# One product 128 rows deep in place of two passes 64 rows deep, in a graph kernel's walk over edge buckets

## The chip, the cores and the metric

The kernel runs on one core of a Trainium2 chip. The metric is the device time of one execution in microseconds (us); of several executions the median is given.

## What is computed

A small graph network over 3125 nodes with 256 features and 53125 directed edges: a message-passing layer, a mixture of expert layers, two averaging graph convolutions, and a last feed-forward layer on selected tokens. Only the first layer matters here:

```python
node_i = node_features[i_idx]
node_j = node_features[j_idx]
msg_input = jnp.concatenate([node_i, node_j, edge_features], axis=-1)
h = jax.nn.relu(msg_input @ mW1 + mb1)
messages = h @ mW2 + mb2
aggregated = jax.ops.segment_sum(messages, i_idx, num_segments=node_features.shape[0])
...
u = jax.nn.relu(update_input @ uW1 + ub1)
updated = u @ uW2 + ub2
return node_features + updated
```

For each edge the hidden vector of 512 elements is a sum of three parts: what the source node gives, what the destination node gives, and what the edge's 16 attributes give.

## The kernel before

A first stage (up to 645 us) sorts the edges into buckets by source node. A bucket is 32 nodes (`BN`), there are 98 buckets (`NBK`), and four buckets make a group. `rows` holds a group's edges, five rounds of 128 edges for each of the four buckets. An edge's row has 68 elements: 32 that mark its source node within the bucket (one of them is 1), 32 for its attributes (16 rounded ones and 16 remainders), and four with indices.

The first stage also makes tables. `tab_b` holds what each node gives as a destination. `tab_h` holds what it gives as a source, split in two halves, `[node, 2, 512]`: a part rounded to the TensorE format float32r, and the remainder. `w_h` holds the attributes' weights, split in the same way. The kernel adds the products with both halves.

The second stage, `edges_by_bucket` (665 to 1860 us), walks 25 groups of five rounds: 125 steps. A step treats four buckets, 128 edges of each:

- `fetch` (L713, GpSimd, called POOL in the profile) gathers each edge's row of `tab_b` into `cb`, one indirect DMA per bucket. It is issued three steps ahead.
- `turned` (L735) turns the first 64 elements of each edge's row on TensorE, so that they lie along the partitions: product with an identity matrix into the PSUM tile `pt`. ScalarE then copies them into `oT` in SBUF (the helper `copy`, L107). It is issued one step ahead of `spread`.
- `spread` (L752) multiplies `oT` with `gives`, a tile that holds the source parts of the bucket's 32 nodes and the 32 rows of attribute weights. The result goes into two PSUM tiles `pa`, two buckets in each. This is where the two passes are: `c` runs over the two halves of the table.
- `hidden_units` (L758, VectorE) adds `pa` to `cb`; `relu` (L763, ScalarE) follows.
- `by_source` (L769) sums the hidden vectors by source node into the PSUM tile `ph`.

Buckets with an even number lie on partitions 0 to 63 of `gives` and `oT`, those with an odd number on partitions 64 to 127. `begin` loads `gives` for the next group, once in five steps, from the SyncE queue; there are two such tiles. The weights' rows of both are loaded once, ahead of the loop (L842).

Between these parts the loop takes one piece at a time of two other jobs: `counts` (one-hot tiles on VectorE at L791 and L795, products at L810, tiles `cn` stored to `adj_h`), and `finish_nodes`, the rest of the layer and the experts for two finished groups of nodes. The latter spans ten steps, so the pattern of the stage repeats every ten. The order on TensorE, VectorE, ScalarE and SyncE is the order written in the program (`manual_schedule`). The PSUM tiles of `turned`, `counts` and `finish_nodes` come in turn from one ring of three banks (`bank`). L506, L521, L524, L531, L546, L556, L619, L635, L639 and L649 are products of `finish_nodes`; L133 is a transpose of it, L777 closes a group.

The remaining stages (from 1860 us) are the two convolutions, with products at L1277, and the last layer.

Of the kernel before, what the change touches and what calls it, by code (L numbers as in the profile page):

```python
# [8 lines left out]
F32 = mybir.dt.float32  # L9
F16 = mybir.dt.float16  # L10
F32R = mybir.dt.float32r
# [5 lines left out]
P = 128  # L17
N, E, D, HID = 3125, 53125, 256, 512
# [5 lines left out]
GB = 4  # L24
# [10 lines left out]
BN, NBK = 32, -(-N // 32)  # L35
# [7 lines left out]
RW = AT_DST + 1  # L43
# [7 lines left out]
def gnn_ffn_kernel(ctx: ExitStack, tc: tile.TileContext, a: dict, out: bass.AP):  # L51
    nc = tc.nc
# [12 lines left out]
    def bank(name):  # L65
        return rings[-1].tile([P, 512], F32, tag="bank", name=name)
# [7 lines left out]
    ident_r = const.tile([P, P], F32R, name="ident_r")  # L74
# [31 lines left out]
    def copy(dst, src):  # L106
        nc.scalar.activation(dst, src, AF.Copy)  # L107
# [40 lines left out]
    tab_h = dram.tile([NP, 2, HID], F32, name="tab_h")  # L148
    w_h = dram.tile([32, 2, HID], F32, name="w_h")
# [311 lines left out]
    def rest_of(fast):  # L461
# [211 lines left out]
        def edges_by_bucket():  # L673
            with tc.tile_pool(name="bk", bufs=2) as bp, tc.tile_pool(name="upd", bufs=2) as up, \
# [5 lines left out]
                for hf, w in ((half0, W0), (half1, W1)):  # L680
                    left = NP - NBK * BN
                    flat = hf[NBK * BN:, :].rearrange("s (h l) -> (s h) l", l=w)
# [4 lines left out]

                gives = [bp.tile([P, 2, 2, HID], F32R, name=f"gives{i}", bufs=1) for i in range(2)]  # L690

                def begin(g):
                    nb = min(4, NBK - 4 * g)
                    ag = gives[g % 2]
                    for i in range(2):
                        src = bass.AP(tensor=tab_h.tensor, offset=tab_h.offset + (g * P + i * BN) * 2 * HID,
                                      ap=[[2 * HID, BN], [4 * BN * HID, nb // 2], [1, 2 * HID]])
                        nc.sync.dma_start(ag[2 * BN * i:2 * BN * i + BN, :nb // 2].bitcast(F32).rearrange("p i c h -> p i (c h)"), src)
                    rows = bp.tile([P, PER, RW], F32R, name="rows", bufs=3)
                    nc.sync.dma_start(rows.bitcast(F32).rearrange("p r w -> p (r w)"),  # L700
                                      cbuf[g * P * PER:(g + 1) * P * PER, :].rearrange("(p r) w -> p (r w)", p=P))
                    return dict(g=g, nb=nb, m=nb * BN, ag=ag, rows=rows, oa={}, ob={})
# [24 lines left out]
                def turned(u, r):  # L727

                    pt = bank("pt")
                    pairs = u["nb"] // 2  # L730
                    flat = u["rows"].rearrange("p r w -> p (r w)")
                    for j in range(u["nb"]):

                        at = (GB * r + j) * RW - j % 2 * 2 * BN
                        nc.tensor.matmul(pt[:, j * P:(j + 1) * P], lhsT=flat[:, at:at + P], rhs=ident_r, start=True, stop=True)  # L735
                    oT = bp.tile([P, 2, P], F32R, name="oT", bufs=2)
                    got = pt.rearrange("p (i k e) -> p i k e", i=2, k=2)
                    for k in range(2):
                        rows = slice(k * 2 * BN, (k + 1) * 2 * BN)
                        copy(oT[rows, :pairs], got[rows, :pairs, k])  # L740
                    return oT

                def spread(u, oT):

                    got = []
                    for j in range(0, u["nb"], 2):
                        pa = pA.tile([P, 2, HID], F32, name="pa")
                        got.append(pa)
                    for c in range(2):
                        for j in range(u["nb"]):  # L750
                            at = slice(j % 2 * 2 * BN, (j % 2 + 1) * 2 * BN)
                            nc.tensor.matmul(got[j // 2][:, j % 2, :], lhsT=oT[at, j // 2, :], rhs=u["ag"][at, j // 2, c, :],  # L752
                                             start=c == 0, stop=c == 1)
                    return got

                def hidden_units(u, cb, pas):
# [72 lines left out]
                def step(i):  # L829
                    g, r = steps[i]  # L830
                    return units[g], r

                def ahead_of(i):
                    if i < len(steps):
                        g, r = steps[i]
                        cbs[i] = fetch(units[g], r)

                units[0] = begin(0)
                for t in gives:
                    for at in (BN, 3 * BN):  # L840
                        for i in range(2):
                            nc.sync.dma_start(t[at:at + 32, i].bitcast(F32), w_h[:])  # L842

# [2 lines left out]
                for i in range(3):  # L848
                    ahead_of(i)
                hs = hidden_units(units[0], cbs[0], spread(units[0], turned(*step(0))))  # L850
                relu(hs, 0), relu(hs, 1)
                leaving(units[0])
                oT = turned(*step(1))
                for i, (g, r) in enumerate(steps):
                    u, more = units[g], i + 1 < len(steps)
                    coming = []
                    if more:
                        v = step(i + 1)
                        coming = hidden_units(v[0], cbs[i + 1], spread(v[0], oT))
# [7 lines left out]
                    if i + 2 < len(steps):  # L867
                        oT = turned(*step(i + 2))
                    take(tally)
                    relu(coming, 1)  # L870
                    if r == 0 and g + 1 < NB:
                        units[g + 1] = begin(g + 1)
# [170 lines left out]
        if fast:  # L1043
            edges_by_bucket()
        else:
            with ExitStack() as es:
                ring(es)
                with tc.tile_pool(name="keys", bufs=1) as kp:
                    edges_by_scatter(kp)
                st["up"] = es.enter_context(tc.tile_pool(name="upd", bufs=2))  # L1050
                for k0, nb in PAIRS:
                    got = []
                    for k in range(k0, k0 + nb):
                        hs = st["up"].tile([P, HW], F32, name="h0")
                        nc.sync.dma_start(hs, hsum[k * P:(k + 1) * P, :])
                        got.append(hs)
                    for _ in finish_nodes((k0, nb), got):
                        pass
            rings.pop()
# [231 lines left out]
        with tc.tile_pool(name="ffn", bufs=2) as fp, tc.tile_pool(name="rank", bufs=1) as rp:  # L1291
            wrow = rp.tile([P, NP], F32, name="wrow")
            for k0, nb in GROUPS:
                pt = bank("ptw")
# [5 lines left out]
            for k in range(NB):  # L1300
                w = wcol[:, k:k + 1]
# [13 lines left out]
            for k0, nb in GROUPS:  # L1315
# [5 lines left out]
                for i in range(nb):  # L1321
                    k = k0 + i
                    py = bank("py")
                    for m in range(8):
                        nc.tensor.matmul(py[:, :D], lhsT=gT[:, m, i * P:(i + 1) * P], rhs=fw2[:, m, :],  # L1325
                                         start=m == 0, stop=m == 7)
# [4 lines left out]
                    rows = min(P, N - k * P)  # L1331
# [50 lines left out]
```

## Time and profile before

| | |
|---|---|
| Time, median of 3 runs | 2401.82 us (2400.23 to 2407.05) |
| Profiled execution: its own time | 2503.9 us |
| Profiled execution: span | 2501.8 us |
| Mean granted TensorE clock over the span | 0.832 |
| PE busy | 1836.7 us (73%) |
| VectorE (DVE) busy | 1549.4 us (62%) |
| GpSimd (POOL) busy | 987.6 us (39%) |
| ScalarE (ACT) busy | 876.3 us (35%) |
| L752, PE | 980 products, busy 188.7 us |
| L735, PE | 490 products |
| L107 oT, ACT | 250 copies, busy 93.1 us, mean 373 ns |

In the profile PE is TensorE, and PEld its loading of the stationary operand. A row reads: source line, engine, operation, tile written and tiles read, shapes, count; then busy time and the mean time of one instruction, from its start to its end. Products overlap in the array, so the busy time of a group divided by its count can be well below the mean of one. In a timeline the first number is the start of a group in us from the start of the span, and the second is the time that it covers. In a list of waits the numbers are the total in us, how many there were, and the longest.

### The profile page before, as it was taken

The numbers are of one execution on the slowest core, as the hardware profiler recorded it, in microseconds if no ns is written. First come the engines' busy times: TensorE is split into PE (matmuls) and PEld (weight loads), VectorE is DVE, ScalarE is ACT, GpSimd is POOL, SyncE is SP. The second block draws the span as 40 slices with busy tenths as digits, with TensorE's granted clock in tenths as the row PEclk, the third lists the DMA queues.
The fourth block names the chain that finished last, engine by engine and source line by source line (L and its number), as shares of the span: only waits on it lengthen the run. The fifth ranks groups of instructions, "written<-read, shape, count | busy, mean of one in ns | idle before, by whom it ended". The sixth has DMA issues, their size and how long they took to land. (4 is left out here: it accounts for less than half of the span.)

```text
span 2501.8 us, 26233 instructions
## 1 busy us (share of the span) xinstructions
PE 1836.7 (73%) x7873; PEld 1091.7 (44%) x7873; DVE 1549.4 (62%) x4427; ACT 876.3 (35%) x1553; POOL 987.6 (39%) x1032
## 2 busy tenths in 40 slices
PE   3455551111078898898898998898885999999689
PEld 1222220000034454455454454454454777886356
DVE  7687775555255665665665665665644676667931
ACT  1211110000045555555555555554433333343111
POOL 4566666766545444445444444444300000110000
PEclk9687775555568889889889899899897999999889
DMA  8233330000666556555555555555304444650000
GB/s 265 96 129 124 119 118 25 25 24 26 167 201 196 146 159 173 161 162 178 157 158 165 150 178 165 149 172 169 114 26 125 120 129 119 169 145 1 0 34 19
DMA packets 231403, 309.98 MB, mean 124 GB/s; under 512 B 34392, under 2 KB 165315, under 8 KB 230884
## 3 DMA queue, kind: packets, MB, share of 16 engines
q1 hardware_dynamic: 167296, 153.00, 20.8%
q0 software_dynamic: 52512, 142.96, 19.6%
q10 hardware_dynamic: 11444, 12.27, 1.6%
q8 instruction: 64, 1.05, 0.2%
q14 instruction: 87, 0.71, 0.1%
HBM read 226.44 MB, written 81.69 MB: 123 GB/s over the span
## 5 line engine op out<-in xcount | busy, mean ns | idle before, releaser
L713 POOL DMA_INDIRECT cb<-tab_b,goes_to x490 | 477.4, 974 | 617.8 <-issue 275.1
L394 POOL DMA_INDIRECT cbuf<-rt,to x416 | 416.3, 1001 | 233.3 <-issue 197.1
L758 DVE TENSOR_TENSOR cb<-pa,cb 128x1024 f32<-128x1024 f32 x245 | 288.7, 1218 | 263.2 <-PE pa L752 190.1
L1277 PE MATMUL padj<-z,slab 128*128 128x512 f32 x1250 | 321.4, 410 | 16.0 <-DVE z L1186 16.0
L763 ACT ACTIVATE cb<-cb 128x1024 f32<-128x1024 f32 x245 | 257.6, 1051 | 94.7 <-DVE cb L758 72.9
L1277 PEld LDWEIGHTS padj<-z,slab 128*128 128x128 f32 x1250 | 233.2, 192 | 75.4 <-issue 24.1
L752 PE MATMUL pa<-gives,oT 64*128 64x512 f32 x980 | 188.7, 506 | 36.1 <-ACT oT L107 34.3
L133 PE MATMUL pt<-ident,xn 128*128 128x128 f32 x200 | 49.5, 339 | 218.8 <-DVE xn L122 130.3
L363 PE MATMUL pk<-oh,later 128*128 128x392 f16 x104 | 47.2, 454 | 190.3 <-DVE oh L340 95.0
L810 PE MATMUL pn<-ob,oa 128*128 128x448 f16 (+1 forms) x692 | 165.6, 363 | 20.6 <-ACT cn L107 7.5
L125 POOL TENSOR_TENSOR x<-x,xn 128x256 f32<-128x256 f32 x25 | 24.4, 978 | 352.7 <-DVE xn L122 352.7
L795 DVE TENSOR_SCALAR ob<-ids,rows 128x448 f16<-128x448 f16 (+1 forms) x490 | 163.3, 333 | 0.0
L791 DVE TENSOR_SCALAR oa<-ids,rows 128x128 f16<-128x128 f16 x692 | 163.0, 262 | 0.0
L752 PEld LDWEIGHTS pa<-gives,oT 64*128 64x128 f32 x980 | 105.8, 231 | 101.2 <-ACT oT L107 43.8
L769 PE MATMUL ph<-cb,rows 128*32 128x512 f32 x980 | 144.8, 645 | 0.0
L107 ACT ACTIVATE oT<-pt 64x256 fp32r<-64x256 f32 (+1 forms) x250 | 93.1, 373 | 134.9 <-DMA cb<-tab_b,goes_to 72.2
L107 ACT ACTIVATE cn<-pn 128x352 f16<-128x352 f32 x196 | 98.3, 502 | 118.0 <-PE pn L810 91.0
L313 PE MATMUL pp<-mw,xTa 128*128 128x512 f32 x200 | 133.1, 826 | 0.2 <-issue 0.2
L133 PEld LDWEIGHTS pt<-ident,xn 128*128 128x128 f32 x200 | 24.8, 160 | 243.1 <-DVE xn L122 129.5
L107 ACT ACTIVATE rt<-row 128x144 f32<-128x144 f32 x104 | 32.8, 319 | 258.7 <-DMA cbuf<-rt,to 208.1
L506 PE MATMUL pd<-xT,fw 128*128 128x512 f32 (+1 forms) x224 | 91.8, 566 | 35.4 <-DVE y L1328 35.4
L735 PEld LDWEIGHTS pt<-ident_r,rows 128*128 128x128 f32 x490 | 67.1, 198 | 110.4 <-issue 69.4
(221 smaller groups left out, 3137.4 us busy)
## 6 DMA issues: line engine op xcount, KB each, us to landing
two<-adj_h SPq DMA_DIRECT2D x24, 1600.0 KB
rows<-cbuf SPq DMA_DIRECT2D x25, 680.0 KB
gives<-tab_h SPq DMA_DIRECT2D x48, 256.0 KB
adj_h<-cn SPq DMA_DIRECT2D x98, 112.0 KB
adj_h<-cn SPq DMA_DIRECT2D x98, 88.0 KB
cb<-tab_b,goes_to POOLq DMA_INDIRECT x490
cbuf<-rt,to POOLq DMA_INDIRECT x416
cbuf<-empty ACTq DMA_DIRECT2D x4, 1632.0 KB
```

The source lines that it names most:

```text
L107: nc.scalar.activation(dst, src, AF.Copy)
L313: nc.tensor.matmul(pp, lhsT=xT[:, c, :], rhs=mw1[:, 2 * h + c, :], start=c == 0, stop=c == 1)
L394: one_of = nc.gpsimd.indirect_dma_start(out=cbuf[:], out_offset=bass.IndirectOffsetOnAxis(ap=to[:n, i:i + 1], axis=0), in_=rt[:n, i, :], i ...
L713: nc.gpsimd.indirect_dma_start(out=cb[:, j, :], out_offset=None, in_=tab_b[:], in_offset=bass.IndirectOffsetOnAxis(ap=u["to"][:, i:i + 1], ...
L752: nc.tensor.matmul(got[j // 2][:, j % 2, :], lhsT=oT[at, j // 2, :], rhs=u["ag"][at, j // 2, c, :], start=c == 0, stop=c == 1)
L758: nc.vector.tensor_tensor(cb[:, j:j + 2], pa, cb[:, j:j + 2], op=OP.add)
L763: nc.scalar.activation(h, h, AF.Relu)
L769: nc.tensor.matmul(u["ph"][j * BN:(j + 1) * BN, :], lhsT=u["rows"][:, GB * r + j, :BN].bitcast(F32), rhs=hs[j // 2][:, j % 2, :], start=r ...
L791: nc.vector.tensor_scalar(oa, ids[:, 1 + i * P:1 + (i + 1) * P], field[:, 0:1], None, op0=OP.is_equal)
L795: nc.vector.tensor_scalar(ob[:, :w], ids[:, 1:w + 1], field[:, 1:2], None, op0=OP.is_equal)
L810: nc.tensor.matmul(pn[:, :w], lhsT=u["oa"].pop((j, r, i)), rhs=u["ob"][j, r][:, :w], start=r == rs[0], stop=r == rs[-1])
L1277: nc.tensor.matmul(pa, lhsT=slab[:, c, :], rhs=(z2 if second else z1)[:, c, :], start=c == 0, stop=c == NB - 1)
```

## The change

The two halves of the source part now lie below each other: the rounded half with its attribute weights on partitions 0 to 63, the remainder half with its own on partitions 64 to 127, for each of the four buckets. `oT` holds a bucket's 64 turned elements twice, once in each half of the partitions. One product 128 rows deep then adds both halves.

```diff
-gives = [bp.tile([P, 2, 2, HID], F32R, name=f"gives{i}", bufs=1) for i in range(2)]
+gives = [bp.tile([P, GB, HID], F32R, name=f"gives{i}", bufs=1) for i in range(2)]
 def begin(g):
     nb = min(4, NBK - 4 * g)
     ag = gives[g % 2]
-    for i in range(2):
-        src = bass.AP(tensor=tab_h.tensor, offset=tab_h.offset + (g * P + i * BN) * 2 * HID,
-                      ap=[[2 * HID, BN], [4 * BN * HID, nb // 2], [1, 2 * HID]])
-        nc.sync.dma_start(ag[2 * BN * i:2 * BN * i + BN, :nb // 2].bitcast(F32).rearrange("p i c h -> p i (c h)"), src)
+    for c in range(2):
+        src = bass.AP(tensor=tab_h.tensor, offset=tab_h.offset + (g * P * 2 + c) * HID,
+                      ap=[[2 * HID, BN], [2 * BN * HID, nb], [1, HID]])
+        nc.sync.dma_start(ag[2 * BN * c:2 * BN * c + BN, :nb].bitcast(F32), src)
...
 def turned(u, r):
     pt = bank("pt")
-    pairs = u["nb"] // 2
-    flat = u["rows"].rearrange("p r w -> p (r w)")
-    for j in range(u["nb"]):
-        at = (GB * r + j) * RW - j % 2 * 2 * BN
-        nc.tensor.matmul(pt[:, j * P:(j + 1) * P], lhsT=flat[:, at:at + P], rhs=ident_r, start=True, stop=True)
-    oT = bp.tile([P, 2, P], F32R, name="oT", bufs=2)
-    got = pt.rearrange("p (i k e) -> p i k e", i=2, k=2)
-    for k in range(2):
-        rows = slice(k * 2 * BN, (k + 1) * 2 * BN)
-        copy(oT[rows, :pairs], got[rows, :pairs, k])
+    nb = u["nb"]
+    for j in range(nb):
+        nc.tensor.matmul(pt[:2 * BN, j * P:(j + 1) * P], lhsT=u["rows"][:, GB * r + j, :2 * BN], rhs=ident_r,
+                         start=True, stop=True)
+    oT = bp.tile([P, GB, P], F32R, name="oT", bufs=2)
+    for c in range(2):
+        copy(oT[2 * BN * c:2 * BN * (c + 1), :nb], pt[:2 * BN, :nb * P].rearrange("p (j e) -> p j e", e=P))
     return oT
 def spread(u, oT):
...
-    for c in range(2):
-        for j in range(u["nb"]):
-            at = slice(j % 2 * 2 * BN, (j % 2 + 1) * 2 * BN)
-            nc.tensor.matmul(got[j // 2][:, j % 2, :], lhsT=oT[at, j // 2, :], rhs=u["ag"][at, j // 2, c, :],
-                             start=c == 0, stop=c == 1)
+    for j in range(u["nb"]):
+        nc.tensor.matmul(got[j // 2][:, j % 2, :], lhsT=oT[:, j, :], rhs=u["ag"][:, j, :], start=True, stop=True)
...
 for t in gives:
-    for at in (BN, 3 * BN):
-        for i in range(2):
-            nc.sync.dma_start(t[at:at + 32, i].bitcast(F32), w_h[:])
+    for c, at in enumerate((BN, 3 * BN)):
+        nc.sync.dma_start(t[at:at + 32].bitcast(F32), w_h[:, c, :].unsqueeze(1).to_broadcast([32, GB, HID]))
```

## The prediction

> **What bounds the kernel now.** The change touches only the stage that walks the buckets of edges, so I looked there first. The windows view, cut at every tenth step of that stage, shows busy time by engine (the next numbers are granted TensorE clock, DMA share and GB/s):
>
> ```profile
> 692.00:757.00 65.00, 48.94 (x222) 23.93 (x222) 36.65 (x73) 31.88 (x50) 31.89 (x34) 0.68 0.65 194
> ...
> 1134.00:1228.00 94.00, 83.83 (x422) 47.45 (x420) 59.19 (x169) 49.20 (x89) 44.33 (x47) 0.90 0.55 167
> ```
>
> Ten steps take 94 us. PE is busy for 83.8 of them, DVE for 59.2, ACT for 49.2, POOL for 44.3. There are eleven such periods from 757 to 1795 us. Then the waits over these periods:
>
> ```profile
> POOL cb L713 <- ACT cb L763: 136.3, 30, 7.3
> DVE cb L758 <- PE pa L752: 136.9, 51, 5.9
> ...
> ACT cn L107 <- PE pn L810: 78.7, 11, 7.7
> ```
>
> DVE and ACT mostly wait for PE, and L752, the changed product, releases the longest of these waits. Only the first ten steps (692 to 757 us) are slack on PE. The chain that ended last is no help: its long pieces start at 1840 us, after this stage.
>
> The timeline of PE is the view that prices the change (start, busy us, then the group):
>
> ```profile
> 1289.54 0.61 PE L810 MATMUL pn<-ob,oa 128*128 128x352 f16 x3
> 1290.08 1.20 PE L752 MATMUL pa<-gives,oT 64*128 64x512 f32 x8
> 1291.21 1.13 PE L506 MATMUL pd<-sh,sw 128*128 128x256 f32 x4
> 1292.18 1.03 PE L506 MATMUL pd<-xT,ew 128*128 128x256 f32 x4
> ...
> 1294.13 0.67 PE L735 MATMUL pt<-ident_r,rows 128*128 128x128 f32 x4
> 1294.64 0.93 PE L810 MATMUL pn<-ob,oa 128*128 128x448 f16 x4
> 1295.50 0.65 PE L619 MATMUL pd<-e,ew 128*64 128x256 f32 x4
> ...
> 1301.85 0.94 PE L810 MATMUL pn<-ob,oa 128*128 128x448 f16 x4
> 1302.62 0.59 PE L635 MATMUL psh<-sw,sh 128*128 128x256 f32 x2
> ```
>
> Eight products of L752 hold PE for 1.13 us (1290.08 to 1291.21), 0.14 us each. The same width at full depth costs more: in the chain view L1277 runs like this,
>
> ```profile
> 2136.80 5.72 PE padj L1277 x25
> ```
>
> 0.229 us each. So the 64-deep products already run two at a time, in the upper and lower half of the array, and **the count of matmuls is not what is saved**. What is saved is the rest of the block.
>
> **What the Trainium skill says.** "TensorEngine Tiling (Array Packing)", Tiling Modes, Key Properties: tiles work in parallel, and changing the tiling mode drains TensorE. The trace agrees with both: the pairs above, and L810 x4 holding PE 0.77 us ahead of the full-width L635 but 0.86 us ahead of the 64-column L619. The page gives no price; 0.09 us is the trace's. "TensorE: Matmul & The Clock Gate", Part 2, step 1: weights load while the running product streams, and their loading depends on the column count, not on depth. The trace agrees: the first L506 group after L752 takes 1.13 us, the next, with its weights loaded ahead, 1.03. The same page, Part 1: idle time halves the TensorE clock. PEclk is 0.88 in most periods, and a block of L752 takes 2.01 us from start to start elsewhere (1339.43 to 1341.44).
>
> **The change part by part**, for one period of ten steps.
>
> 1. L752, 8 products 64 deep become 4 that are 128 deep. Before: 0.09 to 0.10 entry drain, 1.13 for the block and its exit drain, 0.10 for weights that the next group could not load ahead; 1.33 us. After: 4 x 0.229 = 0.92 with neighbours of the same shape. Saving 0.41 us. Where the next group is narrow itself (L769 or L619: three of ten steps) that exit stays, and 0.21 us is saved. Four of ten blocks run at half clock; doubling the clocked parts gives an estimated 0.6 and 0.3 us there. Over one period: three at 0.41, one at 0.37 (behind it come the short L521), two at 0.21, three at 0.6, one at 0.3 = **4.1 us**. Bounds: 2.5 us, if loads are not pulled ahead, to 5.
>
> 2. Order. Now pa of the first two buckets is complete after 6 of 8 products (three pair slots), then after 2 of 4. DVE's L758 starts 0.23 us (0.43 at half clock) earlier, beside the drain saved. This helps the steps where DVE leads; I count it only against item 4.
>
> 3. L735 turns 64 columns instead of 128. Four now take 0.51 us (1294.13 to 1294.64), 0.11 each, as long as a 128-column weight load. The LDWEIGHTS of L619, 64 columns, lasts 134 ns against 192 ns (median, by line), so about 0.055 us apiece, 0.22 for four, is the least. But 64 columns are another mode: PE enters one here already (from L769's 32 columns), but must leave it again: 0.09 plus weights exposed, about 0.08 (0.05 for 64 columns on entry). After L777, one step in five, the entry is new too. Net -0.45 us per period. Bounds: -1.0 (no drain), +1.5 (no shorter products, every drain paid).
>
> 4. oT: two ACT copies of 64x256 become two of 64x512. The price before and the nearest row:
>
> ```profile
> 1337.30 0.78 ACT L107 ACTIVATE oT<-pt 64x256 fp32r<-64x256 f32 x2 [1.46 <-PE pt L521]
> 1338.10 1.06 ACT L763 ACTIVATE cb<-cb 128x1024 f32<-128x1024 f32 x1
> 1339.18 0.60 ACT L107 ACTIVATE hT<-pt 128x512 f32<-128x512 f32 x1
> ```
>
> 0.78 becomes 1.2 us: +0.42 per step, 4.2 us of ACT per period, 49 to 53 us of 94. Mostly it lies beside PE's work: oT is wanted a step later. It shows where PE waits for ACT's queue. The PSUM ring has three banks, so the third group after L735 needs pt's bank back; L524 starts at 1338.13, just as oT ends. Such places per period: L524, L639, L133 after the norm, and L556 after xT (L556 waits 1.7 us). At two of them (L133, L556) the chain runs back through L758 to L752 and item 2 pays. I charge the two others, 0.8, and 0.2 for slack elsewhere in the ring: **+1.0 us**. Bounds: 0.4 to 2.5. Behind the longer copies queue the second relu (L763), cn and xT; L769, POOL's fetch into cb and L810 wait for these, and the relu has most of a step to spare.
>
> 5. SP: gives still comes by two DMAs per group of the same bytes, in pieces of 2 KB instead of 4. They are issued five steps (45 us) ahead; SP's issue took 0.38 us in the median and may double, with nothing but rows and adj_h behind it. Before the loop eight issues of w_h become four. They span 658 to 677 us, but the first oT comes at 691.7, when ACT has issued its last weights. Cost nothing, on that cover; were it gone, 2 us once, either way.
>
> 6. The same store for gives, 2 KB more per partition for oT: no time. The first ten steps go round a loop of L758, relu, oT and L752, 5.9 us a turn: -0.7 at L752 (half clock, first pa early) against +0.4 for oT, about -0.3 each, **-3 us** (0 to -6). The last five steps: -1.
>
> Sum: 11 x (-4.1 - 0.45 + 1.0) = -39; with -3 and -1, **-43 us**. The profiled execution took 2503.9 us (span 2501.8), 102 above the median of 2401.8. No view says where; the granted clock and the order of this stage would have to differ for its share to matter, so I carry the difference over unchanged: 2401.8 - 43 = 2359 us.
>
> **The rivals.**
>
> A. Half the products, half the time: L752 is busy 188.7 us, so -94, to 2308 us. For it: the group's size. Against it: 0.14 us apiece shows that the halves overlap. Chance 0.04.
>
> B. Given back to ACT's queue and the narrow L735. At the upper bounds of items 3 and 4, with 1 at its middle, a period changes by -4.1 + 1.5 + 2.5 = -0.1 us, and the time is 2397 to 2403. For it: three banks only, and ACT's copies run back to back in some steps (oT, cn, relu, cn, xT from 1318 to 1322). Against it: ACT is half idle. Chance 0.10.
>
> C, slower: **the clock**. Less work on PE with the same stalls means longer pauses beside the work, and PE's clock halves after pauses. In the first ten steps, with PE busy 75% by this view, the granted clock is 0.68; in the steady periods, at 89%, it is 0.90. PE's 84 us per period at 0.88 become 84 x 0.88/k. The gain of 3.55 us is gone at k = 0.844; at 0.80 a period costs 8.4 - 3.5 = +4.9 us, and the kernel some 50 more: 2450 us. Against it: what goes is mostly drain, time in which the array did nothing, and no stall is added beyond 0.42 us. Chance 0.11.
>
> **How the numbers follow.** The forecast (2359 us) has a chance of 0.75. Its own range: all of items 1 and 3 at their best, little given back: 11 x -5.0 - 6 = -61, 2341 us; items 3 and 4 near their worst together with 1: about -9, 2393 us. Taking in part of A and B, 2336 to 2396 leaves out some 2 in 10. About 0.3% (7 us) is what a measurement of this kernel can tell from no change: faster 0.79, all of the forecast and A; same 0.09, most of B; slower 0.12, C and the rest.
>
> **What would show it.** Right: L752 x490 with about 0.23 us from start to start, a period of some 90.5 us, L735 with 64 columns at some 0.06 us spacing, oT at 590 to 600 ns, PEclk at 0.87 or higher. Wrong: periods that stay at 94 us with PE waiting for oT at L506, L531 or L810 (B); PEclk under 0.845 in these windows (C); L752 spaced 0.33 us, its weights not loaded ahead.

## The result, and the profile after

| | before | after |
|---|---|---|
| Median of 4 runs each | 2404.14 us (2400.23 to 2407.05) | 2373.35 us (2370.18 to 2379.82) |
| Ratio | | 0.9876, 95% interval 0.9847 to 0.9905 |
| Profiled execution: its own time, span | 2406.98 us, 2404.8 us | 2376.09 us, 2374.0 us |
| Mean granted TensorE clock | 0.843 | 0.856 |

The change made the kernel 30.8 us faster by the medians; 43 were forecast. The profile of before in this table is a second one, taken later (`e0_before_again`): the first, with its span of 2501.8 us, comes from an execution that is no partner for this profile of after, as shown below. After's lines are numbered anew: `turned` is at L732, `spread` at L746, VectorE's add at L751, the relu at L756, `by_source` at L762, `counts` at L803.

The windows view of the kernel after gives the first ten steps and the eleven periods of ten steps together (length; busy time by engine; then granted clock, DMA share and GB/s):

```profile
638.30:691.30 53.00, 38.82 (x183) 17.14 (x183) 36.83 (x73) 34.34 (x48) 31.61 (x34) 0.78 0.78 244
691.30:1671.30 980.00, 845.84 (x4173) 508.26 (x4171) 653.00 (x1857) 579.91 (x979) 488.06 (x516) 0.92 0.58 173
```

The same view of the kernel before, second profile:

```profile
633.80:686.70 52.90, 43.27 (x224) 21.01 (x224) 36.52 (x73) 31.35 (x49) 34.08 (x36) 0.80 0.82 258
686.70:1698.40 1011.70, 918.39 (x4611) 531.74 (x4610) 652.66 (x1857) 540.88 (x979) 488.47 (x517) 0.89 0.57 168
```

Eleven periods took 1011.7 us and take 980.0: **92.0 us per period became 89.1**, and the 31.7 us of all eleven are the whole gain (the stage begins 4.5 us later, the rest of the kernel is 3.7 us shorter, the first ten steps are level). PE's busy time fell by 72.6 us, though, more than twice the gain, and its idle time grew by 40.9 (93.3 to 134.2); ACT's busy time grew by 39. The granted clock rose from 0.89 to 0.92.

The waits view over the eleven periods, after and then before (total us, times, longest):

```profile
DVE cb L751 <- PE pa L746: 130.0, 43, 5.5
...
PEld pt L133 <- ACT oT L107: 49.1, 11, 4.6
```

```profile
DVE cb L758 <- PE pa L752: 160.8, 53, 5.9
...
PEld pt L133 <- ACT oT L107: 39.7, 11, 4.1
```

DVE's wait for `pa` fell from 160.8 us in 53 waits to 130.0 in 43. PE's wait for `oT` at the first transposes after the norm (L133) grew from 39.7 us to 49.1.

The timeline of PE after, the places that priced the change:

```profile
1157.45 0.45 PE L732 MATMUL pt<-ident_r,rows 128*64 128x128 f32 x4
1157.75 0.93 PE L803 MATMUL pn<-ob,oa 128*128 128x448 f16 x4
...
1163.27 0.61 PE L803 MATMUL pn<-ob,oa 128*128 128x352 f16 x3
1163.59 1.22 PE L746 MATMUL pa<-gives,oT 128*128 128x512 f32 x4
1164.65 1.03 PE L506 MATMUL pd<-xT0g,uw 128*128 128x256 f32 x4
1165.51 1.03 PE L506 MATMUL pd<-aT,uw 128*128 128x256 f32 x4
```

From L803's start to that of the second L506 group it takes 2.24 us. Before, the prediction's timeline had 2.64 (1289.54 to 1292.18). So 0.40 us goes per block at full clock. And four turns take 0.30 us from start to start, not 0.50.

### The profile page after: what moved, and what is told of

Same layout as the page of the kernel before. It is cut to its first block, busy times and chain, and to the rows that moved or that the text cites. A ratio compares the mean times of both kernels' runs of the same rounds, so it can differ in the third digit from the quotient of the medians.

```text
span 2374.0 us, 25263 instructions
## 1 busy us (share of the span) xinstructions
PE 1736.6 (73%) x7383; PEld 1056.0 (44%) x7383; DVE 1555.0 (66%) x4427; ACT 918.1 (39%) x1553; POOL 986.0 (42%) x1032
## 5 line engine op out<-in xcount | busy, mean ns | idle before, releaser
L751 DVE TENSOR_TENSOR cb<-pa,cb 128x1024 f32<-128x1024 f32 x245 | 288.5, 1217 | 192.5 <-PE pa L746 176.6
L756 ACT ACTIVATE cb<-cb 128x1024 f32<-128x1024 f32 x245 | 257.8, 1052 | 81.8 <-DVE cb L751 76.4
L133 PE MATMUL pt<-ident,xn 128*128 128x128 f32 x200 | 51.1, 353 | 217.2 <-DVE xn L122 153.4
L746 PE MATMUL pa<-gives,oT 128*128 128x512 f32 x490 | 176.1, 487 | 35.4 <-ACT oT L107 35.2
L107 ACT ACTIVATE oT<-pt 64x512 fp32r<-64x512 f32 (+1 forms) x250 | 144.5, 578 | 91.4 <-DMA cb<-tab_b,goes_to 59.4
L803 PE MATMUL pn<-ob,oa 128*128 128x448 f16 (+1 forms) x692 | 160.0, 351 | 21.3 <-DVE ob L788 8.6
L784 DVE TENSOR_SCALAR oa<-ids,rows 128x128 f16<-128x128 f16 x692 | 169.0, 272 | 0.0
L762 PE MATMUL ph<-cb,rows 128*32 128x512 f32 x980 | 140.1, 622 | 0.0
L133 PEld LDWEIGHTS pt<-ident,xn 128*128 128x128 f32 x200 | 25.6, 166 | 243.3 <-DVE xn L122 143.5
L746 PEld LDWEIGHTS pa<-gives,oT 128*128 128x128 f32 x490 | 102.7, 221 | 68.3 <-ACT oT L107 46.7
L506 PE MATMUL pd<-xT,fw 128*128 128x512 f32 (+1 forms) x224 | 91.6, 565 | 35.4 <-DVE y L1320 35.4
L1196 ACT ACTIVATE slab<-two 128x2048 fp32r<-128x2048 f16 x50 | 95.6, 1911 | 41.4 <-PE padj L1269 39.0
```

The lines of the kernel that those rows point to most:

```text
L506: nc.tensor.matmul(pd[:m, :n], lhsT=w, rhs=v, start=c == 0, stop=c == len(xs) - 1)
L746: nc.tensor.matmul(got[j // 2][:, j % 2, :], lhsT=oT[:, j, :], rhs=u["ag"][:, j, :], start=True, stop=True)
L751: nc.vector.tensor_tensor(cb[:, j:j + 2], pa, cb[:, j:j + 2], op=OP.add)
L756: nc.scalar.activation(h, h, AF.Relu)
L762: nc.tensor.matmul(u["ph"][j * BN:(j + 1) * BN, :], lhsT=u["rows"][:, GB * r + j, :BN].bitcast(F32), rhs=hs[j // 2][:, j % 2, :], start=r ...
L784: nc.vector.tensor_scalar(oa, ids[:, 1 + i * P:1 + (i + 1) * P], field[:, 0:1], None, op0=OP.is_equal)
```

## Experiments

Theory 1: PE sets the pace in only about half of the steps of a period; there the saved time passes through, elsewhere it turns into waits for ACT's copies, which are longer now. Its rivals: the longer copies alone hold the gain back, or PE's time passes through in full and some other edit costs time. The runs fell on four chips. On the first (e0 to e3) the kernel before takes 2407 us, about as in the result above; on the second (e4 to e7) 2488, on the third (e8, `e7_half_passes_again`) 2491, on the fourth (`e5_one_copy_again`, `e7_half_passes_again2`) 2485. The kernels on one chip share the runs of the kernel before there, and each ratio is read against these.

**The kernel before, once more** (`e0_before_again`, no edit).

> The kernel before, unchanged. It gives a second profile of it and the width of a comparison that should come out at 1.000. Theory 1 (the profile shown of before was an odd execution): its second stage starts near 640 us, not 692, and a period of ten steps takes 91 to 92 us instead of 94.3, since 11 periods at 2.5 us less make the measured gain of 30 us. Rival (the first profile was typical of the second stage): the period is 94 us again, and the 55 us that the stage gained in the two profiles are lost elsewhere.

2406.66 us, ratio 1.0001 (0.9988 to 1.0014), span 2404.8. The second stage starts at 633.8 us and a period takes 92.0, as theory 1 of this run had it. The first profile's extra 100 us belonged to the chip or the execution.

**The order alone** (`e1_order`): the kernel before, with both passes of two buckets ahead of those of the other two.

```diff
-for c in range(2):
-    for j in range(u["nb"]):
+for c, j in [(c, j + k) for j in range(0, u["nb"], 2) for c in range(2) for k in range(2)]:
```

> The kernel before, with the eight 64-deep products of a step in the order of the pairs, so that the first pa is complete after 2 of 4 slots instead of 3 (item 2 of the prediction alone). If VectorE's start is what counts: 0.23 us in each of the few steps that VectorE leads, 3 per period, some -8 us (0.997). If TensorE alone counts: 1.000.

2397.68 us, 0.9957 (0.9943 to 0.9972): -10 us. DVE's wait for `pa`, 160.8 us before, fell most of the way to the changed kernel's 130.0 (waits view, up to 1680 us):

```profile
DVE cb L758 <- PE pa L752: 138.5, 55, 5.4
```

In the profiled execution the eleven periods take 993.5 us, 18.3 less than before's 1011.8, but the stage begins 7.6 us later, at 641.3, though the edit touches nothing ahead of it. So how much the order alone is worth within the stage is less sure than the -10 of the whole time.

**The narrow turn alone** (`e2_narrow_turn`): the kernel before with L735 turning 64 columns, and both copies reading the 64 partitions that this fills.

```diff
-at = (GB * r + j) * RW - j % 2 * 2 * BN
-nc.tensor.matmul(pt[:, j * P:(j + 1) * P], lhsT=flat[:, at:at + P], rhs=ident_r, start=True, stop=True)
+nc.tensor.matmul(pt[:2 * BN, j * P:(j + 1) * P], lhsT=u["rows"][:, GB * r + j, :2 * BN], rhs=ident_r,
+                 start=True, stop=True)
...
-    copy(oT[rows, :pairs], got[rows, :pairs, k])
+    copy(oT[rows, :pairs], got[:2 * BN, :pairs, k])
```

> The kernel before, with L735 turning 64 columns instead of 128, and the copies at their old size (item 3 alone). By the prediction -0.45 us per period, -5 us (0.998), as leaving the 64-column form would drain TensorE. By the trace after, where the next group starts 0.06 us behind the last narrow product and four take 0.30 us instead of 0.50: -0.2 us in each step, -2.1 per period, up to -23 us (0.990).

2404.52 us, 0.9994 (0.9983 to 1.0006): -1.4 us, not to be told from nothing. Yet each step's turn is 0.20 us shorter on PE (1072.55 to 1072.85 for four). Where it goes shows in PE's timeline of the kernel before, second profile, one step on:

```profile
1066.31 0.38 PE L524 MATMUL pdeg<-ident,hsb 128*1 128x128 f32 x2 [0.47 <-ACT oT L107]
...
1071.91 0.66 PE L735 MATMUL pt<-ident_r,rows 128*128 128x128 f32 x4
1072.41 0.93 PE L810 MATMUL pn<-ob,oa 128*128 128x448 f16 x4
...
1077.62 0.70 PE L506 MATMUL pd<-aT,uw 128*128 128x256 f32 x2 [0.43 <-DVE aT L534]
```

In this step PE waits 0.43 us for DVE's copy anyway. A turn that ends 0.2 us earlier makes that wait longer. Only two steps of ten became shorter by 0.2 us (9.3 to 9.1 and 8.5 to 8.3).

**The longer copies alone** (`e3_long_copies`): the kernel before, each `oT` copy taking all four buckets' columns.

```diff
-oT = bp.tile([P, 2, P], F32R, name="oT", bufs=2)
-got = pt.rearrange("p (i k e) -> p i k e", i=2, k=2)
+oT = bp.tile([P, GB, P], F32R, name="oT", bufs=2)
+got = pt.rearrange("p (j e) -> p j e", e=P)
...
-    copy(oT[rows, :pairs], got[rows, :pairs, k])
+    copy(oT[rows, :2 * pairs], got[rows, :2 * pairs])
...
-    nc.tensor.matmul(..., lhsT=oT[at, j // 2, :], rhs=u["ag"][at, j // 2, c, :], ...)
+    nc.tensor.matmul(..., lhsT=oT[at, j, :], rhs=u["ag"][at, j // 2, c, :], ...)
```

> The kernel before, with both oT copies made 64x512 instead of 64x256, the added half unused (item 4 alone). By the prediction +1.0 us per period, +11 us (1.005). If the copies are what ate the rest of the gain, +2.5 us per period or more, +28 us (1.012). If ScalarE's queue has slack everywhere: 1.000.

2417.36 us, 1.0051 (1.0033 to 1.0069): +12 us. The copies grew from 377 to 589 ns (groups view), 0.42 us per step, and the price shows at the places where PE's timeline waits for the ring: L524 now waits 1.14 us where it waited 0.47 (the profile puts the wait down to DVE's copy of L524's earlier result, which frees a bank of the same ring). The profiled execution was the fastest of the six, 2410.7 us, at a granted clock of 0.852 against 0.843, and its periods took only 2.5 us more in all; where the rest of the +12 arises it does not show.

Lengths of the ten steps of a period (from one step's first L752 or L746 to the next one's, median of eleven periods, single records of the trace), first chip and after:

| step | 0 | 1 | 2 | 3 | 4 | 5 | 6 | 7 | 8 | 9 |
|---|---|---|---|---|---|---|---|---|---|---|
| before (e0) | 8.2 | 5.4 | 10.8 | 9.3 | 8.3 | 8.6 | 7.9 | 8.5 | 13.0 | 12.0 |
| order (e1) | 7.7 | 5.5 | 10.8 | 9.3 | 8.4 | 8.5 | 7.9 | 8.5 | 11.7 | 11.2 |
| narrow turn (e2) | 8.3 | 5.4 | 10.7 | 9.1 | 8.3 | 8.5 | 8.0 | 8.3 | 13.1 | 12.0 |
| long copies (e3) | 7.6 | 6.0 | 10.8 | 9.3 | 8.3 | 8.5 | 8.8 | 9.0 | 12.6 | 12.0 |
| after | 7.7 | 5.8 | 10.6 | 8.7 | 7.8 | 9.1 | 8.0 | 8.3 | 11.6 | 11.0 |

The order gives at steps 0, 8 and 9. The product adds steps 3 and 4, which no partial edit but the turn's 0.2 us had moved. The long copies take back at 1, 6 and 7 when they come alone, and after has a loss of its own at step 5.

The following runs are from the three other chips.

**After, once more** (`e4_after_again`, no edit).

> The changed kernel, unchanged, for a narrower interval and as the base for the three other runs of this call. Both theories: 0.987, -31 us.

2482.22 us where the kernel before took 2487.89: 0.9983 (0.9962 to 1.0004). **On this chip the gain is almost gone.** Steps 3 and 4 are 8.7 and 7.8 us as above, but step 2 takes 13.4 us instead of 10.6 (in a profiled execution of 2491.8 us, 10 above the median). ACT, DVE and PE in that step (timelines of `e4_after_again`):

```profile
1059.06 0.60 ACT L107 ACTIVATE hT<-pt 128x512 f32<-128x512 f32 x1 [1.20 <-PE pa L746]
```

```profile
1060.50 0.28 DVE L525 COPY deg<-pdeg 1x128 f32<-1x128 f32 x1 [2.24 <-PE pagg L531]
```

```profile
1054.78 0.62 PE L521 MATMUL pt<-ident,hsb 128*128 128x128 f32 x4
1056.83 0.38 PE L524 MATMUL pdeg<-ident,hsb 128*1 128x128 f32 x2 [1.43 <-ACT oT L107]
...
1059.70 1.99 PE L531 MATMUL pagg<-hT,mw 128*128 128x256 f32 x8 [0.97 <-issue]
```

`hT` copies what L521 had finished at 1055.4, `deg` what L524 had finished at 1057.2; both start only at 1059.06 and 1060.50. The releasers named are not what the instructions read. In after's own profile the same two run without a pause, at 1153.21 and 1153.62. What holds two engines back here the trace does not show.

**One copy** (`e5_one_copy`): after, with each bucket turned into both halves of `pt`, so that one copy of 128x512 does. These are eight float32 products; the profile has two records for each.

```diff
 for j in range(nb):
-    nc.tensor.matmul(pt[:2 * BN, j * P:(j + 1) * P], lhsT=u["rows"][:, GB * r + j, :2 * BN], rhs=ident_r, ...)
+    for c in range(2):
+        nc.tensor.matmul(pt[2 * BN * c:2 * BN * (c + 1), j * P:(j + 1) * P],
+                         lhsT=u["rows"][:, GB * r + j, :2 * BN].bitcast(F32), rhs=ident, ...)
 oT = bp.tile([P, GB, P], F32R, name="oT", bufs=2)
-for c in range(2):
-    copy(oT[2 * BN * c:2 * BN * (c + 1), :nb], ...)
+copy(oT[:, :nb], ...)
```

> The changed kernel, but TensorE writes each bucket's 64 turned elements into both halves of pt (16 products of float32 instead of 4 of float32r, two at a time in the two column halves), so that one ScalarE copy of 128x512 (0.6 us) does what two of 64x512 do (1.2 us). If ScalarE's queue and the ring of three banks eat the gain, some 12 us are won back, or 20 if the copies cost more beside the shorter products: 0.979 to 0.982. If TensorE alone counts, the added products (0.2 to 0.4 us per step) cost 25 us or more: 0.997 or above.

2479.02 us, 0.9961 (0.9943 to 0.9978). PE's and ACT's timelines (here of the second run, below):

```profile
1155.48 1.09 PE L733 MATMUL pt<-ident,rows 128*64 128x128 f32 x16
```

```profile
1156.71 0.60 ACT L107 ACTIVATE oT<-pt 128x512 fp32r<-128x512 f32 x1 [0.69 <-PE pt L733]
```

PE pays 1.03 us from start to start (1055.13 to 1056.16 in another period) in place of 0.30, ACT 0.60 instead of 1.20. Step 5 falls from 9.1 to 7.5 us and step 2 from 13.4 to 11.0, steps 3 and 4 grow by 0.7 and 0.6. So the loss at step 5 goes when the second copy goes; the long copies alone had not caused it (8.5 us in e3). The ratio fits neither outcome that was expected, 0.979 to 0.982 or 0.997 and above.

**The wide turn kept** (`e6_wide_turn`): after, with the turn of 128 columns.

```diff
-nc.tensor.matmul(pt[:2 * BN, j * P:(j + 1) * P], lhsT=u["rows"][:, GB * r + j, :2 * BN], rhs=ident_r, ...)
+at = (GB * r + j) * RW
+m = min(P, PER * RW - at)
+nc.tensor.matmul(pt[:m, j * P:(j + 1) * P], lhsT=flat[:, at:at + m], rhs=ident_r, ...)
```

> The changed kernel, but L735 turns 128 columns again (64 of them unused), the copies as changed: item 3 undone alone. If TensorE's time counts fully, +0.2 us per step, +2.1 per period, +23 us: 0.997. If that time falls into waits for ScalarE, as in the kernel before with the narrow turn alone (-1.4 us): 0.987 to 0.989.

2494.5 us, 1.0020 (0.9997 to 1.0042). Against the kernel after on the same chip (e4) that is 12.3 us more, between medians of 22 runs each, whose single times scatter by 7 to 9 us (standard deviation). So the wide turn costs the changed kernel some 10 us here, about half of the 23 that PE's time would make, where the narrow one alone (e2) had brought 1.4. Steps 3 and 4 are 0.2 and 0.1 us longer than in e4, and steps 0 and 1 together by 2.0; the granted clock of the runs is lower, 0.832 against 0.841 (medians).

**One pass of two** (`e7_half_passes`): the kernel before with `for c in range(1)` and `start` and `stop` always true. It leaves out the products with the remainders.

> The kernel before with the remainder half's pass left out: four products of 64 rows per step instead of eight, in two pair slots instead of four, the loads and the other parts as before (the sums lack the remainders). TensorE gets 0.46 us less work per step, 4.6 per period, 6 with the half clock, and the first pa is ready after 1 slot of 3. If TensorE's time passes through in full: -50 to -66 us (0.973 to 0.979). If about half of it turns into waits for ScalarE and VectorE, as the sums of the first four runs suggest: -30 us (0.987).

2488.35 us, 1.0001 (0.9981 to 1.0021), on the chip of e4. Run again on the third chip:

> The kernel before with the remainder half's pass left out, once more, since in the last call the kernel before took 2488 us and hardly any kernel differed from it. Where the kernel before takes some 2406 us: full passage of TensorE's 0.46 us per step gives -50 to -66 us (0.973 to 0.979), half of it lost to waits gives -30 us (0.987). Where it takes some 2488 us: 1.000 as before.

2483.69 us, 0.9969 (0.9944 to 0.9994). And on the fourth:

> The kernel before without the second pass of L752; leaves out the remainder half of the source parts and its attribute weights. It takes four 64-deep products per step off PE, some 0.55 us at full clock, keeps the mode drains and the 64x256 copies. Theory 1 (PE sets the pace in about half of the steps, as in the changed kernel): where the kernel before takes about 2406 us, 11 periods of -2.5 to -3.5, -28 to -38 us, 0.984 to 0.988. Rival (PE's time passes through in full, what was given back in the changed kernel is the copies'): 11 x -6, -60 to -66 us, 0.973 to 0.975. Where the kernel before takes about 2488 us, 0.996 to 1.000 by both, since the third step of each period waits for its gathers instead.

2491.41 us, 1.0028 (1.0013 to 1.0044). Three chips, and a change of at most 0.3% either way, where full passage would have given 0.973 to 0.979 and half 0.987 (for the third and fourth chip about 1.000 had been expected either way). Steps 3, 4 and 9 take 8.8, 7.9 and 11.1 us, and step 2 takes 12.4, 13.0 and 14.9; in the first profile of before, the only one of that kernel with the longer time, these steps took 9.3, 8.4 and 12.0, and step 2 11.7. So what the kernel saves in some steps it loses in step 2 even with half the products gone. The granted clock fell as well: 0.825, 0.828 and 0.825 (medians of the runs) against the kernel before's 0.837 to 0.838. That PE's time doesn't pass through in full on these chips is shown; the waits of theory 1 aren't tested by it, and it says little on the first chip, where step 2 has no such gap.

**The second copy on VectorE** (`e8_vector_copy`): after, `nc.vector.tensor_copy` for `c = 1`.

> The changed kernel, but the second of the two oT copies is made by VectorE (tensor_copy, 64x512), so ScalarE has 0.6 us less in each step and TensorE the same work. If ScalarE's queue and the PSUM bank that it holds eat the gain: 10 to 20 us faster than the changed kernel, 0.979 to 0.983 where the changed kernel is at 0.987 (0.990 to 0.994 where it is at 0.998). If VectorE is as short of time as ScalarE, or its copy waits behind the one-hots: no gain, or up to 10 us slower than the changed kernel.

2485.38 us where before took 2491.21: 0.9979 (0.9958 to 1.0000), level with after on the chip of e4; the 10 to 20 us that were expected of a relieved ScalarE did not come. The copy itself, by the groups view:

```profile
L736 DVE CAST oT<-pt 64x512 fp32r<-64x512 f32 x113 | 77.3, 684 | 61.7 <-ACT oT L107 56.2 <-issue 3.7 <-ACT cb L757 0.5
```

Step 5 falls to 8.2 us, step 2 rises to 14.5 in this execution.

**One copy, once more** (`e5_one_copy_again`).

> The changed kernel with 16 products of L733 (pairs into both halves of pt) and one oT copy of 128x512 in place of two of 64x512, once more. Theory 1: the second copy on ScalarE costs the changed kernel some 12 us (what e3 cost the kernel before), and the 16 products give back 0.7 us in two steps of ten (11 x 1.4 = 15 us), while step 5 gains 1.6 (18 us). Where the kernel before takes about 2406 us in this call: 2365 to 2375 us, a ratio of 0.983 to 0.988, level with the changed kernel's 0.987. Rival: the copies are what holds the changed kernel back, then 0.978 to 0.982. Where the kernel before takes about 2488 us: 0.995 to 0.998 by both.

2475.85 us where before took 2485.07: 0.9961 (0.9939 to 0.9983), the same ratio on a second chip. Its lead over after (0.9983 on one of these chips) lies within both intervals. It is the best version there; on the first chip it wasn't tried.

## Why the prediction was right, and where it was off

**The direction held, the mechanism in part, and the size partly by luck.** 2373 us lies in the range, 14 us above the forecast. PE does bound enough of the stage, and a shallower block of time in it shortens some steps by just what it saves: steps 3 and 4, which run at full clock, lose 0.60 and 0.56 us, and block and turn together had saved 0.40 + 0.20. But over the period other steps give back 0.9 us (steps 1, 5 and 6), and 2.1 of the 2.9 us gained come at steps 8 and 9 (means of the eleven periods). There the granted clock comes in, which the sum had left as it was. Step 8 of the kernel before (second profile) in two periods, then of the kernel after in two, by the windows view:

```profile
1397.22:1410.29 13.07, 12.30 (x53) 6.49 (x52) 10.62 (x25) 4.77 (x9) 7.07 (x8) 0.81 0.56 162
1489.35:1501.06 11.71, 10.58 (x52) 5.18 (x52) 9.92 (x24) 4.76 (x9) 6.91 (x8) 0.99 0.61 178
```

```profile
847.15:860.57 13.42, 11.77 (x49) 6.21 (x48) 11.50 (x25) 5.40 (x10) 7.12 (x8) 0.84 0.54 156
938.88:950.29 11.41, 10.09 (x50) 5.02 (x48) 9.90 (x24) 5.40 (x10) 6.82 (x8) 1.00 0.63 192
```

The first number after the window is its length, the third from the end the granted clock. In both kernels the step takes 12.9 to 13.8 us when a part of it runs at half clock, and 11.2 to 11.9 when none does. By the trace's clock records 10 of the 11 periods of before have such a part in step 8, 5 of e1's, 2 of after's. The step's mean falls from 13.06 to 11.88 us: **13 of the 31.7 us come with the clock at this one step**. The block that opens step 9 takes 2.08 us in before (1134.38), and 1.2 in nine of after's eleven periods. In the four runs of after the mean granted clock was 0.851 to 0.857, in 30 runs of before on the first chip 0.842 to 0.851. Why the clock stays up there is open. So a gain that the sum did not have made up for waits that it had put too low.

With the ratios of the first chip times 2404 us, and the result, the terms compare like this:

| | forecast | measured |
|---|---|---|
| item 1 with 2: the product and its order | -45 | -41, by difference |
| of it the order alone (e1) | not summed | -10 |
| item 3: the narrow turn (e2) | -5 | -1.4 |
| item 4: longer copies (e3) | +11 | +12.3 |
| first ten steps, last five | -4 | 0 and at most -3.7 (profiles) |

The difference -29.8 + 1.4 - 12.3 = -41 (-29.8 is the result by its ratio) assumes that the parts add up; the intervals leave some 9 us on it either way. And the parts need not add up: the turn, 1.4 us alone, is worth some 10 in the changed kernel (e6, on another chip).

**Item 1** was priced well on PE at full clock: 0.40 us per block against 0.41. Before the narrow L762 0.20 goes (1.41 to 1.22 us, from L803's last start to L762's second), where 0.21 was forecast. At half clock step 0 saves 0.59 against 0.6 (3.52 to 2.93 us over three groups), step 6 only 0.39. How the 0.40 is made up also came out as told. Single records of before have 0.24 us from L810's last product to the block, where L810's own spacing is 0.15; 0.34 to the block's second pair, where the later pairs follow at 0.23; 0.33 from the last pair to L506; and 0.32 to L506's second product, where 0.22 is usual. These four delays of about 0.1 us are the saving. In after the starts from L803's last product to L506's second are the usual ones, but for the block's first product, which starts 0.12 us early and so makes the block's 1.06 us look longer than 0.92.

**Item 2** was called useful only against item 4. Alone it brings 10 us, at steps 0, 8 and 9; at step 8 this goes with the clock, and what an early first `pa` gives by itself was not separated from that. With -10 for it in the sum, the 128-deep product itself brings about -31. By the periods of the profiles (order -18.3, turn -3.8, copies +2.5, all together -31.8) it would be only -12. The runs leave that open.

**Item 3 failed twice, in opposite directions.** I charged a drain and exposed weights for leaving the 64-column turn, because entering L619 cost 0.09. The trace shows none: L803 starts 0.30 us after the turn and holds PE 0.77 us ahead of L506 (1167.76 to 1168.53), as it did before (1083.25 to 1084.02). "TensorEngine Tiling (Array Packing)", Tiling Modes, Key Properties, on which I had leaned, says that a change of tiling mode drains TensorE; at this place no run shows it. So a period saved 2.0 us of PE instead of 0.45, more than my best case of 1.0. And of these 2.0 us e2 let only 0.13 through. The step that failed is to count PE's time as the kernel's in all ten steps.

**Item 4** was right in size by e3's time, for a cause close to the one given: L524, behind the turn, waits until the copies out of `pt` are done. L524 waits 1.42 us after, 0.47 before:

```profile
1152.27 0.38 PE L524 MATMUL pdeg<-ident,hsb 128*1 128x128 f32 x2 [1.42 <-ACT oT L107]
...
1185.05 0.44 PE L133 MATMUL pt<-ident,xn 128*128 128x128 f32 x2 [1.86 <-ACT hsb L107]
1187.48 1.87 PE L556 MATMUL pgate<-gw,xT 128*128 128x4 f32 x8 [2.00 <-ACT xT L107]
```

and ACT's timeline of after says why: the copies stand behind a relu, and end at 1152.21, just ahead of it.

```profile
1150.07 1.06 ACT L756 ACTIVATE cb<-cb 128x1024 f32<-128x1024 f32 x1 [0.60 <-DVE cb L751]
1151.03 1.18 ACT L107 ACTIVATE oT<-pt 64x512 fp32r<-64x512 f32 x2
```

Where I had let item 2 pay for L133 and L556, it did not: they wait 1.86 and 2.00 us, against 1.42 and 1.71 before, and step 5 grew by half a microsecond. Over the eleven periods PE's idle time grew by 40.9 us while its busy time shrank by 72.6. The forecast had 11 of waits and 50 of work. Turns that end early and now wait could account for 11 x 1.9 = 21 us of the waits, if e2's share held in the changed kernel, which e6 puts in doubt.

**Item 5** (nothing) stands. **Item 6**: the first ten steps took 52.9 us and take 53.0. A loop through L752 that PE's saving and `oT`'s cost would shorten by 3 us does not show; what sets their pace instead is open (PE is busy for 38.8 of 53 us, DMA at 0.78).

**The rivals.** A is out: the 490 products of L746 keep PE busy for 176.1 us in all (page of after), the 980 of L752 for 182.6 (page of the second profile). B was right in its mechanism for 12 us by e3, nearly a third of what items 1 and 2 brought by difference. C pointed the wrong way for this change: the clock rose to 0.92 with less work in the block. In e7, with half the products gone, it did fall, from 0.837 to 0.825. I had also carried the first profile's extra 100 us over unchanged. The stage in it had periods of 94.4 us against 92.0 in the second; steps 1 and 2 were longer there, as in e4 on the second chip. If it came from such a chip, which the record does not say, the change is worth 0.2% there by e4, 0.4% at most, and my sum fitted the chip that I had not seen better than the one whose trace I read: luck again.

**What stays open**: why the kernel takes 80 us more on three of the chips. Its second stage begins some 45 to 65 us later there, ACT's longest wait for the scatter of the first stage is 9.0 to 10.2 us instead of 5.4 and 5.8, and step 2 has the gap that e4 shows. That DMAs land later there is likely and not shown. Open too is what keeps the clock up in step 8, and with it how much of the gain is the product's and how much the order's.

## What to carry to other kernels

Price a saving on the bounding engine step by step: where that engine already waits in a step, a shorter piece of it only lengthens the wait, and in the kernel before nearly all of the 2 us that shorter turns saved per period went that way. In the changed kernel the same turn was worth some 10 us: measure a part within the whole, too. Look at the granted clock step by step before a gain is put down to work that went: here 13 of 31.7 us came with it at one step. Two half-deep passes that already run side by side are worth merging for the drains and exposed weights around them, and for the earlier first result, not for the count of products. Watch what the merge asks of its inputs: doubling the operand over the partitions cost some 12 us by e3, at least in part through a ring of three banks, though the engine that copies was half idle.

## What the runs showed that I had not expected

Leaving a 64-column group of products for a full-width one cost nothing where these products run one by one: L803 follows the last turn of after by 0.064 us, and the turns each other by 0.060. It cost 0.10 us where they run in pairs, in e5: 0.205 us to L803, with 0.109 from pair to pair. The two products of such a pair start 0.007 us apart, so the halves of `pt` are filled side by side; yet a pair of records takes nearly as long as two single turns (0.109 against 0.120). They are float32 where the single ones are float32r, and no run separates that. The same kernel pair gives 0.988 on one chip and 0.998 on another. And in before and after alike step 8 takes 13 us or 11.5, as a part of it runs at half clock or not.
